# Edge layer of a four-layer graph network: GpSimd's gathers may run three groups of four columns ahead of TensorE's transposes instead of four

## The chip, the cores and the metric

The kernel runs on one core of one Trainium2 chip, in one launch. The metric is the device time of the whole program in microseconds (us). The kernel before takes 7771.75 us, the median of ten runs (7759.88 to 7787.9).

## What is computed

A graph has 12500 nodes with 32 features and 400000 edges, sorted by their target node (`dst`). Four layers run one after the other, each followed by adding its input and a layer normalisation. The change is in the third layer, which works on edges:

```python
rol, col = (edge_index[0], edge_index[1])
e_feat = jnp.concatenate([x[rol], x[col], edge_attr], axis=-1)
h = jax.nn.relu(e_feat @ W1 + b1)
v = h @ W2 + b2
x_cand = jax.ops.segment_max(v, col, num_segments=num_nodes)
return jnp.maximum(x_cand, x[:, -v.shape[-1]:])
```

So every edge needs the 32 features of its source node (random rows of a table), the 32 features of its target node (the same for a run of neighbouring edges, as they are sorted), and 32 features of its own. Then comes a small network (96 to 64 to 32), and the maximum over the edges of one target. The other three layers are sums over edges; this kernel does them as products with a dense count matrix `A`, in fp8.

## The kernel before

Edges lie as 128 partitions x 3125 columns, so that one column is 128 edges. The first 308 columns (edges of the 'heavy' targets) are treated apart, 98 blocks of them, by a generator called `heavy` (lines 1333 to 1453). The other 2817 columns are the work of `edge_layer` (line 1501 on). It takes them in three parts (`cuts`: 1984, 508 and 325 columns), each part in batches of 48 columns, each batch in **groups of four columns**. There are 705 groups; this text counts groups from 0, so group n holds the gathers number 4n+1 to 4n+4.

What a group needs, by engine and line:

- **POOL** (GpSimd) gathers the source rows, one indirect DMA for each column (`fetch`, which calls the helper at line 110): `ef<-table,ids`, 128 rows of 128 bytes. Nothing else gathers; the same engine also has to gather the results of finished parts (`ends<-scan,end_i`, 98 of them, line 110 too).
- **DVE** (VectorE) spreads the target's features over the batch with 32 scans (line 1582), and **ACT** (ScalarE) copies the edge features in (line 1578), once for each batch and one batch ahead.
- **PE** (TensorE) transposes the four columns (line 1705), DVE copies the result out of PSUM (`eT<-pT`, line 1707), PE runs the first product (lines 1736 and 1738), ACT the ReLU (line 1741), PE the second product (line 1754), ACT copies the result to `v` (line 1756).
- When a batch is through, DVE takes the running maximum with 32 scans (line 1591), and SP writes them out (`scan<-o`, 768 KB, line 1594). The next batch but one then loads `attr` (line 1562) and `begin` (line 1565), 768 KB each.

How far POOL may run ahead is set by hand. The indices of a gather are not read from `rows` directly, but from a small copy of four columns, `ids` (line 1683, on DVE). `allow` makes that copy. `AHEAD` copies are made before the loop; after that, each group's copy `eT` is followed on DVE by one further `ids` copy, that of the group `AHEAD` places later. A gather waits for its `ids`, so POOL can be at most `AHEAD` groups in front of the copy `eT`:

```python
def allow():
    if groups:
        e, k = groups.pop(0)
        ids = small.tile([P, 4], I32, name="ids", bufs=AHEAD + 2)
        nc.vector.tensor_copy(ids[:, :k], rows[:, e:e + k])
        allowed.append(ids)
...
            behind = nc.vector.tensor_copy(eT[:, :k], pT[:3 * D, :k])
            with tc.issue_after(behind.ins):
                allow()
            fill(0)
```

`fill` (called twice for each group) puts other work between: up to three steps of `heavy` for each group until its 98 blocks are done (lines 1387 to 1452; a block has its own place in every engine's queue, four groups apart), and later steps of `round_part`, that is products of the last layer with `A` (line 1320, 832 KB loads of `A` by SP). These run for nodes that the finished first or second part has already settled.

A tile framework sets the order of instructions on each engine and the semaphores. It orders by its own estimate of when things are ready; the order on an engine is then fixed, and an instruction that waits holds up all behind it on its engine.

When a part's last batch is through, `end` gathers and writes back 128 boundary rows (`fx`, `fix`), after `LEAD` further groups, and `done` gathers the `ends` and finishes nodes.

Of the kernel before, what the change touches and what calls it, by code (L numbers as in the profile page):

```python
# [119 lines left out]
def dense_path(ctx, tc, bad_i, x, src, dst, edge_attr, w1T, w1_b, w2, w2T, w2_b, aT,  # L120
# [1125 lines left out]
    with ExitStack() as st:  # L1246
# [102 lines left out]
        def heavy(hidden, outer):  # L1349
# [28 lines left out]
            for b in range(H):  # L1378
# [72 lines left out]
                for j in range(4):  # L1451
                    nc.vector.scalar_tensor_tensor(most, got[:, j, :D], lack[:, j:j + 1], most,
                                                   op0=OP.add, op1=OP.max)

        edge_layer(tc, ident, cuts, heads, edge_attr, m_W1, m_b1, m_W2, table, scan, starts_d,
                   rows_d, cont_d, psum, done, fill, lambda *a: first.append(heavy(*a)))
        while fillers:
# [43 lines left out]
def edge_layer(ctx, tc, ident, cuts, heads, edge_attr, m_W1, m_b1, m_W2, table, scan, starts_d,  # L1501
# [13 lines left out]
    C = E // P  # L1515
    HE = P * cuts[0]
    T = 48
    AHEAD = 4
    LEAD = 2 * AHEAD
    HID = m_W1.shape[1]  # L1520

    const = ctx.enter_context(tc.tile_pool(name="e_const", bufs=1))
# [79 lines left out]
    def end(s, last):  # L1602
# [30 lines left out]
        nc.scalar.copy(carry, po[:, :D])  # L1633
        yield from range(LEAD)
        fx = small.tile([P, D], F32, name="fx", bufs=1)
# [43 lines left out]
# [7 lines that stand above are left out]
    begin(lambda B, eT: hidden(nc, psum, small, mw1, mb1, B, 0, 4, eT),  # L1686
          lambda ready: outer(nc, psum, mw2, *ready))
    for _ in range(AHEAD):
        allow()
# [59 lines left out]
def outer(nc, psum, mw2, B, t, k, hT):  # L1749
    HID = P // 2  # L1750
    pv = psum.tile([P, 2, 2, D], F32, name="pv")
    if k == 4:
        for j in range(2):
            nc.tensor.matmul(pv[:, j].rearrange("p h d -> p (h d)"), hT[:, j, :], mw2,  # L1754
                             start=True, stop=True)
        nc.scalar.copy(B.v[:, t:t + 4, :].rearrange("p (h j) d -> p j h d", h=2), pv)
    else:
        for j in range(k):
            q = slice((j // 2) * HID, (j // 2 + 1) * HID)
            nc.tensor.matmul(pv[:, j % 2, j // 2, :], hT[q, j % 2, :],  # L1760
                             mw2[q, (j // 2) * D:(j // 2 + 1) * D], start=True, stop=True)
            nc.scalar.copy(B.v[:, t + j, :], pv[:, j % 2, j // 2, :])
# [660 lines left out]
```

## Time and profile before

| | |
|---|---|
| median of ten runs | 7771.75 us |
| the profiled execution | 7779.74 us |
| its span (first to last instruction) | 7777.9 us |
| edge layer: first gather of `ef` starts, last one ends | 2936.1 and 6599.4 us |
| stretch with `heavy` beside the groups | about 2936 to 4917 us |
| two stretches with products of the last layer beside the groups | within 5800 to 6280 and 6375 to 6600 us |

The profile's page gives each engine's busy time, the span in 40 slices of 194 us (a digit is the busy share in tenths; PEclk is the clock that was granted to TensorE, in tenths of full speed), and groups of instructions by line with their idle time before them and what ended it. Further views are the table by stretches of time, the list of waits, and the timeline, in which a row is: start, duration, engine, line, operation, tiles written and read, and in brackets how long the engine sat idle and what released it. For an indirect DMA, POOL's busy time is the making of its descriptors; the data lands later. 'issue' is a gap that no other engine explains.

### The profile page before, as it was taken

The numbers are of one execution on the slowest core, as the hardware profiler recorded it, in microseconds if no ns is written. First come the engines' busy times: TensorE is split into PE (matmuls) and PEld (weight loads), VectorE is DVE, ScalarE is ACT, GpSimd is POOL, SyncE is SP. The second block draws the span as 40 slices with busy tenths as digits, with TensorE's granted clock in tenths as the row PEclk, the third lists the DMA queues.
The fourth block names the chain that finished last, engine by engine and source line by source line (L and its number), as shares of the span: only waits on it lengthen the run. The fifth ranks groups of instructions, "written<-read, shape, count | busy, mean of one in ns | idle before, by whom it ended". The sixth has DMA issues, their size and how long they took to land. (4 is left out here: it accounts for less than half of the span.)

```text
span 7777.9 us, 196882 instructions
## 1 busy us (share of the span) xinstructions
PE 6710.3 (86%) x85600; PEld 5344.6 (69%) x85600; DVE 3935.2 (51%) x11040; ACT 1636.3 (21%) x3386; POOL 3514.0 (45%) x3445
## 2 busy tenths in 40 slices
PE   6788999898999997888888888678669979799998
PEld 4678999888999994555555555333335636799998
DVE  6999898795443124555555555433343343411122
ACT  1334788100000002222222222211112212100000
POOL 1003410000565527777777777777777776100000
PEclk7889999999999996767777676555569959999999
DMA  1138444889999982222222222211127726699998
GB/s 50 64 132 323 184 201 198 301 331 339 334 356 353 359 334 84 59 58 55 59 54 63 55 55 58 58 52 54 48 74 239 244 74 201 217 347 364 350 358 303
DMA packets 575180, 1447.57 MB, mean 186 GB/s; under 512 B 108408, under 2 KB 269792, under 8 KB 560864
## 3 DMA queue, kind: packets, MB, share of 16 engines
q1 hardware_dynamic: 433200, 1347.10, 47.2%
q0 software_dynamic: 110240, 66.25, 4.2%
q10 hardware_dynamic: 30864, 21.54, 0.9%
q8 instruction: 673, 11.03, 0.6%
q14 instruction: 203, 1.65, 0.1%
HBM read 1155.33 MB, written 279.27 MB: 184 GB/s over the span
## 5 line engine op out<-in xcount | busy, mean ns | idle before, releaser
L110 POOL DMA_INDIRECT ef<-table,ids x2817 | 2674.2, 949 | 884.6 <-issue 635.7
L369 PE MATMUL y<-x,a 128*128 128x96 bf16 x49980 | 2255.8, 206 | 112.9 <-issue 76.3
L369 PEld LDWEIGHTS <-a 128*128 128x128 fp8e4 x49980 | 2174.0, 98 | 142.6 <-issue 99.6
L1705 PE MATMUL pT<-ident,ef 128*96 128x128 f32 x2817 | 772.8, 357 | 571.3 <-DMA ef<-table,ids 551.6
L1705 PEld LDWEIGHTS pT<-ident,ef 128*96 128x96 f32 x2817 | 398.9, 162 | 1030.1 <-DMA ef<-table,ids 684.7
L1707 DVE COPY eT<-pT 96x512 f32<-96x512 f32 x705 | 476.1, 675 | 1065.5 <-PE pT L1705 1065.4
L983 PE MATMUL pa<-oh,ol 128*128 128x196 bf16 x4928 | 726.1, 270 | 120.3 <-DVE oh L973 77.0
L1754 PEld LDWEIGHTS pv<-mw,hT 128*128 128x128 f32 x3208 | 600.4, 261 | 266.7 <-issue 94.7
L989 ACT ACTIVATE at<-pa 128x784 uint16<-128x784 f32 x816 | 647.2, 824 | 504.9 <-PE pa L983 477.7
L277 DVE TENSOR_REDUCE v<-y 128x128 f32<-128x384 f32 (+2 forms) x152 | 83.5, 549 | 1270.5 <-PE y L271 1270.2
L1754 PE MATMUL pv<-mw,hT 128*128 128x64 f32 x3208 | 681.5, 350 | 21.0 <-ACT hT L1741 14.2
L1741 ACT ACTIVATE hT<-ph,mb 128x256 f32<-128x256 f32 x802 | 380.9, 475 | 1336.6 <-PE ph L1738 1310.0
L1019 PE MATMUL y<-x,at 128*128 128x102 bf16 x9604 | 644.8, 209 | 9.9 <-DVE x L257 5.4
L983 PEld LDWEIGHTS <-ol 128*128 128x128 bf16 x4928 | 552.5, 149 | 133.6 <-issue 78.3
L1736 PE MATMUL ph<-eT,mw 96*64 96x256 f32 x1410 | 632.7, 542 | 12.0 <-DVE eT L1707 10.6
L1738 PE MATMUL ph<-eT,mw 96*64 96x256 f32 x1408 | 632.2, 543 | 0.0
L973 DVE TENSOR_TENSOR oh<-bins_h,pl 128x1568 bf16<-128x1568 bf16 x616 | 601.1, 976 | 0.0
L1019 PEld LDWEIGHTS <-at 128*128 128x128 fp8e4 x9604 | 559.1, 98 | 23.1 <-issue 10.9
L110 POOL DMA_INDIRECT g<-code_d,ws_i x25 | 202.4, 8097 | 804.4 <-DVE ki L760 541.1
L115 POOL DMA_INDIRECT sorted_d<-hrow,pos x308 | 370.5, 1203 | 373.0 <-issue 203.6
L1320 PE MATMUL y<-a,x 128*96 128x512 fp8e4 (+1 forms) x1950 | 494.7, 390 | 1.3 <-DVE x L257 1.2
L968 DVE TENSOR_TENSOR ol<-la,lb 128x1024 bf16<-128x1024 bf16 x616 | 425.7, 693 | 72.1 <-PE pa L983 71.7
(406 smaller groups left out, 7019.2 us busy)
## 6 DMA issues: line engine op xcount, KB each, us to landing
a<-A SPq DMA_DIRECT2D x245, 3136.0 KB
A<-at SPq DMA_DIRECT2D x98, 1568.0 KB
a<-A SPq DMA_DIRECT2D x144, 832.0 KB
ef<-table,ids POOLq DMA_INDIRECT x2817
starts_d<-rows SPq DMA_DIRECT2D x44, 1024.0 KB
attr<-in_edge_attr SPq DMA_DIRECT2D x57, 768.0 KB
begin<-starts_d SPq DMA_DIRECT2D x57, 768.0 KB
scan<-o SPq DMA_DIRECT2D x57, 768.0 KB
```

The lines of the kernel that those rows point to most:

```text
L110: return nc.gpsimd.indirect_dma_start(out=o, out_offset=None, in_=tab, in_offset=IndirectOffsetOnAxis(ap=idx, axis=0))
L369: nc.tensor.matmul(y[:, q, :], block(h, q - q0), x3[:, h, :3 * F], start=(q + h == first), stop=False)
L973: nc.vector.tensor_tensor(oh, bins_h[:, None].to_broadcast([P, 4, HJ, 2]), pairs(pl[:, t, 0, half * 64 + w0:half * 64 + w0 + 8])[:, :, Non ...
L983: nc.tensor.matmul(pa[:, 2 * b + i, :HJ], ols[t][:, :, :, 4 * u + 2 * b + i].rearrange("p a b -> p (a b)"), ohs[t][:, 2 * u + b, :, i], st ...
L989: nc.scalar.activation(at[:, qd, :, off:off + 8].rearrange("p h (w j) -> p h w j", w=4), pa[:, :, :HJ].rearrange("p w (h j) -> p h w j", h ...
L1019: nc.tensor.matmul(y[0][:, q, :], at[:, q - 2 * half, h, :], x3[:, h, :3 * F0], start=(q + h == 0), stop=(c < EARLY and last and q == 2 * ...
L1320: nc.tensor.matmul(y[:3 * D, :nq * Q], x3[:, h, :3 * D], a[:, :nq, h - h0, :], start=(h == lo), stop=(h == hi - 1))
L1705: nc.tensor.transpose(pT[:3 * D, j, :], B.ef[:, t + j, :], ident)
L1707: behind = nc.vector.tensor_copy(eT[:, :k], pT[:3 * D, :k])
L1736: nc.tensor.matmul(ph[:HID, :ka], mw1, eT[:, :ka], start=True, stop=True)
L1738: nc.tensor.matmul(ph[HID:2 * HID, :k - 2], mw1, eT[:, 2:k], start=True, stop=True)
L1754: nc.tensor.matmul(pv[:, j].rearrange("p h d -> p (h d)"), hT[:, j, :], mw2, start=True, stop=True)
```

## The change

One constant goes from four to three; a second one, which was derived from it, is written out so that it stays at eight:

```diff
     T = 48
-    AHEAD = 4
-    LEAD = 2 * AHEAD
+    AHEAD = 3
+    LEAD = 8
     HID = m_W1.shape[1]
```

`AHEAD` is used in two places: the ring of `ids` buffers (`AHEAD + 2`, now five instead of six) and the number of `allow` calls before the loop (three instead of four). So the `ids` copy that follows group n's `eT` on DVE is that of group n+3 instead of n+4. No instruction is added or removed in the edge layer's arithmetic, and as many gathers are made. As the framework orders by its own estimate, the order changes with it in some places, which the built programs show: on PE 392 of 392 products of line 1447 (a late step of `heavy`) stand one to three transposes earlier than before, on POOL the `fx` gathers of the first two parts and the first eleven `ends` gathers stand four column gathers earlier, and on SP some `scan<-o` stores stand ahead of the `attr` load that they followed. On DVE the order of `eT`, `ids` and the steps of `heavy` is the same in all but a few places.

## The prediction

> **What bounds the kernel now.** I read the page's slices first, then the groups by line, then the waits of POOL, then the timeline around one batch. The page shows where the edge layer lies, and that POOL looks only three quarters busy in it:
>
> ```profile
> POOL 1003410000565527777777777777777776100000
> PEclk7889999999999996767777676555569959999999
> ```
>
> The group of the column gathers says what the other quarter is:
>
> ```profile
> L110 POOL DMA_INDIRECT ef<-table,ids x2817 | 2674.2, 949 | 884.6 <-issue 635.7
> ```
>
> A gather takes 0.949 us, and 0.314 us (884.6 / 2817) pass before each, of which most is released by nothing. That is 1.25 us for a column and 5.0 us for a group, whatever else runs: from 2936.1 to 4921.5, POOL starts 395 groups at 5.03 us each. So from 2936 to some 5960 us **POOL is the bound**, without slack: what delays a gather there delays the end. The table by stretches shows where it isn't (columns: PE, PEld, DVE, ACT, POOL busy, PEclk, DMA share, GB/s):
>
> ```profile
> 2936.00:4917.00 1981.00, 1660.87 (x8704) 1039.26 (x8705) 1072.31 (x4239) 514.10 (x1338) 1500.66 (x1577) 0.71 0.22 59
> 4917.00:5530.00 613.00, 460.86 (x1475) 227.87 (x1474) 233.46 (x932) 105.96 (x266) 463.34 (x492) 0.50 0.20 53
> 5960.00:6185.00 225.00, 225.00 (x1290) 137.88 (x1290) 84.42 (x342) 48.35 (x118) 159.70 (x170) 1.00 0.77 248
> 6480.00:6600.00 120.00, 120.00 (x713) 76.45 (x713) 40.12 (x154) 24.19 (x56) 81.11 (x86) 1.00 0.68 213
> ```
>
> In the last two rows PE is busy all the time: there PE is the bound, and POOL waits at the gate (`ids`).
>
> **The change.** It adds and removes no work. It moves one release: the `ids` that follow the copy `eT` of group n on DVE now let POOL start group n+3, not n+4. I priced it by asking of each group: when did POOL start it, and when would its `ids` have been there one place later? At the slowest place of a batch the timeline of DVE has
>
> ```profile
> 4104.36 0.68 DVE L1707 COPY eT<-pT 96x512 f32<-96x512 f32 x1
> 4105.11 0.34 DVE L1683 COPY ids<-rows 128x4 int32<-128x4 int32 x1
> 4109.72 0.69 DVE L1707 COPY eT<-pT 96x512 f32<-96x512 f32 x1 [0.87 <-PE pT L1705]
> 4110.33 0.15 DVE L1683 COPY ids<-rows 128x4 int32<-128x4 int32 x1
> ```
>
> and that of POOL
>
> ```profile
> 4103.26 0.94 POOL L110 DMA_INDIRECT ef<-table,ids  x1 [0.30 <-issue]
> ...
> 4108.26 0.94 POOL L110 DMA_INDIRECT ef<-table,ids  x1 [0.31 <-issue]
> ```
>
> Counted from the first, the `eT` copies are those of groups 229 and 230, and the gathers are the first ones of groups 232 and 233. With four ahead, the two `ids` copies release groups 233 and 234, 2.8 us early. With three ahead they are the release of 232 and 233, and come 2.2 us after POOL wanted to start (4105.45 against 4103.26; 4110.48 against 4108.26). Where POOL does wait for `ids`, it starts 0.27 us after the copy ends; so POOL loses 2.2 + 0.27 = 2.5 us here, once: the second shortfall is covered by the first.
>
> Why `eT` is late there, PE's timeline says: at the seam of two batches the 768 KB transfers `attr` and `scan<-o` start at 4086.3 and 4086.8, and the columns of group 228 land late.
>
> ```profile
> 4091.43 0.45 PE L1705 MATMUL pT<-ident,ef 128*96 128x128 f32 x1 [4.17 <-DMA ef<-table,ids]
> 4093.83 0.45 PE L1705 MATMUL pT<-ident,ef 128*96 128x128 f32 x1 [1.96 <-DMA ef<-table,ids]
> ```
>
> The last column's descriptors were done at 4087.98 and PE had it at 4093.83, 5.85 us later. PE's clock falls to 0.50 in it (from 4089 to 4110), and PE needs the next eight groups to catch up. So the shortfall comes once in a batch of 12 groups, that is 60 us.
>
> *Sum, first stretch.* Over all groups of the 33 batches beside `heavy`, start of group n against end of the `ids` copy that will be its release: in 30 batches POOL would be held, by 0.27 us more than the largest shortfall in the batch (from 0 to 2.55 us); the 30 sum to **48 us**. All of it counts only if PE, DVE and ACT are delayed with POOL; where they keep their pace, a late POOL finds the next release early. What they have in reserve is read from the time between a group's last gather and its `eT`: 1.7 to 1.8 us is the shortest in the trace (then they wait for POOL), and 13 of the 33 batches reach under 2 us, 19 under 2.7. PE waits for gathers 129 times for 260 us in this stretch, so they do follow POOL. Carrying the delay from group to group (POOL takes over the delay of its release plus the shortfall; the copies take over POOL's delay less their reserve above 1.8 us) leaves 34 us; above 2.7 us it would be 57 us; counting only the 13 batches that surely follow, 26 us. I take 41, between 34 and 48.
>
> *From 4917 to 5530* `heavy` is gone and the copies come early: the smallest reserve at three ahead is 1.56 us. Nothing. *From 5530 to 5960* 98 − 20 `ends` gathers are shared with POOL, and two groups fall short at a batch's seam, by at most 1.6 us: with the carried reserve 3 us. *5960 to 6185*: PE sets the pace, 5.2 us a group; the queue between POOL and PE gets shorter by a group (`eT` follows the last gather by 15 to 16 us there, so 10 us would be left, against 1.8 needed). Nothing inside. But when PE gets free at 6185 and POOL is the bound again, POOL is one group less far: 5.6 us, on the path. *6480 to 6600*: PE bound again to the last group; POOL's lead is worth nothing there. Nothing. After that the program is the same.
>
> *What else moves.* Five `ids` buffers instead of six: a copy waits for the gather five groups back, long done, and costs nothing. `LEAD` stays. Behind a gather that waits on POOL stand only more gathers. On DVE nothing new waits. PE's order is changed: products of line 1447 stand one or two transposes earlier. At the seam two transposes (0.32 us each) move behind them and one product of line 1736 (0.69 us) moves ahead of the last: `eT` of group 229 is between 0.6 us earlier and 0.7 later, so 33 batches make −20 to +23 us. I take nothing, as `eT` of 230, with the same shortfall, has the same order ahead of it.
>
> Sum: 41 + 3 + 5.6 = **50 us**. Against the profiled execution, 7779.74 + 50 = 7830; that execution lies 8 us above the median of the ten runs, so the time is 7771.75 + 50 = **7822 us**.
>
> **A rule that speaks against a loss.** The row is the 5.85 us above, from a column's descriptors to PE. The Trainium skill, page "DMA: Bandwidth & Descriptors", section "Anatomy of one DMA", gives a DMA from GpSimd about 2.0 us of fixed time. By that rule alone three groups in front are ample, and the sum would be nothing. The measured number decides.
>
> **Rivals.**
> 1. *No difference (within 15.5 us).* The gate binds, but not for long: PE, DVE and ACT keep their pace, so that one shortfall of some 2.8 us (2.55 + 0.27) makes room for all later ones, and with the lead lost at 6185 it is 2.8 + 5.6 = 8 us: 7780. For it: 14 batches never come under 2.7 us. Against it: PE's 260 us of waiting.
> 2. *Not slower, even faster.* The place is PE in the stretches where it is the bound and DVE's `lack` (line 1450), which waits 485 us for line 1447. If 1447, moved ahead of transposes that wait for columns, brings `eT` more than 2.5 us earlier at the seam, the gate never binds there; and POOL's waits for `ids`, 115 of 55.6 us, go down to the usual 0.30 us, which gives 21 us: 7751. It decides from 2.5 us on; I found at most 0.6.
> 3. *More.* POOL's hold makes PE idle just where it now catches up, and its clock stays at half for longer. The granted clock around here stands in stretches of 6.8, 13.7 and 20.5 us, so 3.4 us looks like its step; one more step at half in each batch costs PE 1.7 us, 33 x 1.7 = 56 us: 50 + 56 = 106, or 7878. With the upper carry (16 more) and the later `eT` (23 more) it is 7917. For it: beside `heavy` the mean clock is 0.71, so half-clock is common. Against it: the carried delays leave PE as busy per batch as before.
> 4. *The change doesn't do what it says*, as POOL never needs more than three groups: 30 batches speak against it; it would give 7772.
>
> **Chances.** A measurement of this kernel tells 0.2%, 15.5 us, from no change. Forecast (slower by 16 to 90 us) 0.70; rival 3 and what else lies beyond that 0.09; rival 1, with 4, 0.14; rival 2 0.07. So faster 0.07, same 0.14, slower 0.79. The range: its lower end is the least carry with the best order of transposes (26 − 20 = 6 us, 7777; rival 1's 7780 lies above it), its upper end rival 3 without the further terms (7878, rounded to 7880); some 0.18 is left out.
>
> **What would show it.** In the changed kernel's profile, the first stretch should be some 41 us longer (395 groups at 5.13 us instead of 5.03); POOL's waits for DVE's `ids` should grow from 115 to some 200, with waits of 1 to 2.5 us once in 60 us beside `heavy`; 4917 to 5530 should be as long as now; the tail after the last gather too. I am wrong if the waits grow but the stretch doesn't (rival 1), if `eT` at the seam comes earlier by over 1 us (rival 2), or if PE's mean clock beside `heavy` falls under 0.71 by more than 0.02 (rival 3).

## The result, and the profile after

| | before | after |
|---|---|---|
| median | 7774.28 us (30 runs) | 7833.0 us (9 runs) |
| ratio | | 1.0077, 95% interval 1.0068 to 1.0086 |
| profiled execution, span | 7777.9 us | 7829.8 us |
| edge layer: group 0 to group 395 starts | 1985.4 us | 2040.1 us |
| group 395 to 530 | 694.5 us | 694.3 us |
| copy of the last group after the first gather | 3683.7 us | 3741.8 us |

The change costs 58.7 us on the medians; a second timing of both gave 1.0071 (1.0058 to 1.0085). The two profiled executions differ by 52 us only, as the work ahead of the edge layer happened to end 9.7 us earlier in the one after (the first gather starts at 2926.4 instead of 2936.1). From the first gather on, the copy of the last group comes 58.1 us later.

The page of the kernel after, the busy slices of POOL, the clock and the group of the column gathers:

```profile
POOL 1003410000565427777777777777777776100000
PEclk7889999999999997766676677555569959999999
L110 POOL DMA_INDIRECT ef<-table,ids x2817 | 2672.5, 949 | 950.8 <-issue 667.4
```

POOL's work is the same (949 ns a gather); its idle time before gathers grew by 66 us (950.8 against 884.6). The table by stretches says where, cut at group 395 as the prediction's rows of before are, to within one group:

```profile
2926.00:4966.00 2040.00, 1724.24 (x8713) 1063.08 (x8715) 1078.82 (x4247) 513.95 (x1339) 1501.98 (x1581) 0.70 0.21 57
4966.00:5580.00 614.00, 513.74 (x1484) 240.90 (x1480) 236.47 (x939) 106.79 (x269) 464.06 (x493) 0.50 0.19 53
```

The first row holds one group more than the row 2936 to 4917 of before (1581 against 1577 instructions on POOL); counted between the same gathers, the stretch takes 55 us longer. The second is as long as before. POOL's waits in the first stretch, before and then after (columns: us in total, times, longest):

```profile
POOL ef L110 <- DVE ids L1683: 10.7, 35, 0.3
```

```profile
POOL ef L110 <- DVE ids L1683: 81.8, 100, 3.9
```

Before, an `ids` copy was never late beside `heavy` (no wait over the usual 0.3 us). After, 100 gathers wait for it, and 71 us more in all. Most of the 100 are waits of the usual 0.3 us that some other row had before. Read gather by gather, 32 waits exceed 0.45 us, and what they have above the usual 0.3 us sums to 56.6 us, about what the stretch grew by. They lie in 19 of the 33 batches, nearly all at the first gather of a batch's fifth or sixth group; the other 14 batches lose nothing.

The seam shown in the prediction looks like this afterwards. POOL, then DVE:

```profile
4118.90 0.94 POOL L110 DMA_INDIRECT ef<-table,ids  x1 [0.31 <-issue]
4122.69 0.94 POOL L110 DMA_INDIRECT ef<-table,ids  x1 [2.84 <-DVE ids L1683]
...
4127.90 0.94 POOL L110 DMA_INDIRECT ef<-table,ids  x1 [0.52 <-DVE ids L1683]
```

```profile
4112.37 0.15 DVE L1683 COPY ids<-rows 128x4 int32<-128x4 int32 x1
4121.50 0.69 DVE L1707 COPY eT<-pT 96x512 f32<-96x512 f32 x1 [1.37 <-PE pT L1705]
4122.26 0.15 DVE L1683 COPY ids<-rows 128x4 int32<-128x4 int32 x1
4126.87 0.69 DVE L1707 COPY eT<-pT 96x512 f32<-96x512 f32 x1 [0.86 <-PE pT L1705]
4127.48 0.15 DVE L1683 COPY ids<-rows 128x4 int32<-128x4 int32 x1
```

The gather at 4122.69 is the first of group 232, the one that the prediction named. It waits 2.84 us, of which 0.3 are usual: 2.5 us are lost. The next group, at 4127.90, loses 0.2 more. The copies are late because columns are, as before; PE's timeline at the seam (group 228):

```profile
4109.93 0.45 PE L1705 MATMUL pT<-ident,ef 128*96 128x128 f32 x1 [4.63 <-DMA ef<-table,ids]
```

Which batches are held goes with how late columns are: the last column of the batch's first group reaches PE 5.3 us after its descriptors were done in the 19 (3.0 to 6.1), and 1.9 us in the others (1.3 to 4.0; batch 0 left out, means and extremes).

One thing is different at the seam: the order on PE. The end of group 229's four transposes, before and then after:

```profile
4101.31 1.75 PE L1447 MATMUL z<-ends,last 128*128 128x33 f32 x8
4102.88 1.04 PE L1393 MATMUL y<-one,key 128*128 128x128 bf16 x8
4103.72 0.42 PE L1705 MATMUL pT<-ident,ef 128*96 128x128 f32 x1
```

```profile
4119.40 0.63 PE L1705 MATMUL pT<-ident,ef 128*96 128x128 f32 x2
4119.96 1.12 PE L1736 MATMUL ph<-eT,mw 96*64 96x256 f32 x2
4121.01 0.45 PE L1705 MATMUL pT<-ident,ef 128*96 128x128 f32 x1
```

A product of line 1736 (two records, 1.12 us at half clock) now stands ahead of the group's last transpose. From the last transpose of group 228 to that of group 229 PE takes 11.1 us, where it took 9.9 before (4109.93 to 4121.01; 4093.83 to 4103.72). It is 11.1 us in each of the 19 held batches, and was 9.9 us in each of the 16 batches of before whose last column took over 4 us.

### The profile page after: what moved, and what is told of

The parts are those of the page before. It is cut to its first block, busy times and chain, and to the rows that moved or that the text cites. A ratio compares the mean times of both kernels' runs of the same rounds, so it can differ in the third digit from the quotient of the medians.

```text
span 7829.8 us, 196864 instructions
## 1 busy us (share of the span) xinstructions
PE 6817.8 (87%) x85600; PEld 5372.1 (69%) x85600; DVE 3940.5 (50%) x11040; ACT 1635.8 (21%) x3386; POOL 3510.7 (45%) x3445
## 5 line engine op out<-in xcount | busy, mean ns | idle before, releaser
L110 POOL DMA_INDIRECT ef<-table,ids x2817 | 2672.5, 949 | 950.8 <-issue 667.4
L1705 PE MATMUL pT<-ident,ef 128*96 128x128 f32 x2817 | 803.4, 361 | 521.3 <-DMA ef<-table,ids 517.7
L1754 PEld LDWEIGHTS pv<-mw,hT 128*128 128x128 f32 x3208 | 619.4, 267 | 289.3 <-issue 102.9
L1754 PE MATMUL pv<-mw,hT 128*128 128x64 f32 x3208 | 716.2, 359 | 29.9 <-ACT hT L1741 24.0
L1736 PE MATMUL ph<-eT,mw 96*64 96x256 f32 x1410 | 641.3, 549 | 9.8 <-DVE eT L1707 8.9
L1738 PE MATMUL ph<-eT,mw 96*64 96x256 f32 x1408 | 642.0, 550 | 0.0
```

The source lines that it names most:

```text
L110: return nc.gpsimd.indirect_dma_start(out=o, out_offset=None, in_=tab, in_offset=IndirectOffsetOnAxis(ap=idx, axis=0))
L1705: nc.tensor.transpose(pT[:3 * D, j, :], B.ef[:, t + j, :], ident)
L1736: nc.tensor.matmul(ph[:HID, :ka], mw1, eT[:, :ka], start=True, stop=True)
L1738: nc.tensor.matmul(ph[HID:2 * HID, :k - 2], mw1, eT[:, 2:k], start=True, stop=True)
```

## The experiments

The **theory** is that of the prediction: three groups in front are too few at the seams of the batches beside `heavy`, because 1.5 MB of transfers there make columns land late and PE then works at half clock, and too few by a group at the end of the first stretch where PE is the bound. The **rivals** are that the changed order of instructions costs the time; that the seam's own work, and not the transfers, makes the copies late; and that a longer lead always helps, or a shorter one always costs. The first four kernels, and the last four, ran on chips where the kernel before takes 7773 and 7777 us. The four between ran on a chip where it takes 9067 us.

**Two groups.** Edit: `AHEAD = 2`, `LEAD = 8`.

> AHEAD = 2, LEAD stays 8. Theory (late release at the seams): the shortfalls of the kernel before, read with two groups of lead, are up to 11.5 us where three groups gave up to 2.55 beside heavy, and even the median group is short. Carried from group to group as in the prediction, with a reserve counted above 1.8 us or above 2.7 us, the end is 259 to 328 us later than with four; so 8030 to 8105 us, with most of it (213 to 268 us) before the group 395. Rival (the changed order of instructions costs the time, and the release itself little): no rule says that the order gets steadily worse, so about what three ahead cost, 7800 to 7870 us.

Measured: 8050.12 us, ratio 1.0355 (1.0336 to 1.0374), 277 us more. Up to group 395 the stretch is 210 us longer, at the last copy 266 us. The end is where the carried shortfalls put it (259 to 328, near the lower end), the stretch 3 us short of its range (213 to 268). A cost that steps from 0 to 59 to 277 us, as the shortfalls read from the trace of the kernel before say, speaks for the release. It doesn't exclude the order by itself, as the order moves too: the products of line 1447 stand five to seven transposes earlier here than before.

**Three and a half groups.** The `ids` of a group are copied in two halves, each with its own place in the queue of releases (against the kernel after; the main lines):

```diff
-    AHEAD = 3
+    AHEAD = 7
...
-            e, k = groups.pop(0)
-            ids = small.tile([P, 4], I32, name="ids", bufs=AHEAD + 2)
-            nc.vector.tensor_copy(ids[:, :k], rows[:, e:e + k])
+            e, k, o = groups.pop(0)
+            if o == 0:
+                held[:] = [small.tile([P, 4], I32, name="ids", bufs=6)]
+            ids = held[0][:, o:o + k]
+            nc.vector.tensor_copy(ids, rows[:, e:e + k])
...
-                allow()
+                for j in range(0, k, 2):
+                    allow()
```

> The release goes by half groups of two columns, seven halves ahead, so POOL may be three and a half groups in front. Theory (late release): half a group is 2.5 us of POOL's time, and the largest shortfall at three groups was 2.55 us, so beside heavy almost every shortfall is gone: the stretch up to group 395 takes within 8 us of what it took with four ahead, and at the end of the stretch where PE is the bound half of 5 us is lost: 7774 to 7786 us. Rival (the order): the order lies between those of three and four groups, and the time with it, about 7795 to 7815 us.

Measured: 7784.73 us, 1.0014 (1.0004 to 1.0023), 12 us more; up to group 395, 9.9 us more. The time is in the theory's range and the stretch 2 us over it. Half a group, 2.5 us of POOL's time, brings back 47 of 59 us. The rival's 7795 is excluded by the interval (its upper end is 7791). But the rival's condition didn't come about: the order at the seam is that of four groups here (776 of the 784 records of line 1447 stand where they stood before). So this run took away late release and changed order together, and can't tell one from the other.

**No loads of `attr`, with three groups and with four.** The features of the first batch's edges are used for all batches, so both leave out 56 of 57 loads:

```diff
-            self.at = work.tile([P, T, D], F32, name="attr", bufs=1)
-            nc.sync.dma_start(self.at.rearrange("p t d -> p (t d)")[:, :n * D],
-                              of_stage(edge_attr, s)[:, cols])
+            self.at = attr0
```

> AHEAD = 3, and the edges' own features are loaded once for the first batch and used for all batches, so 56 of the 57 loads of 768 KB are left out (the computation of the other batches uses the wrong features). Theory (the transfers at the seam make the columns land late, and only there is the release late): half of the burst of 1.5 MB is gone, some 3.5 us of it at 214 GB/s, more than any shortfall, so beside heavy at most a fifth of the 55 us remains: 7774 to 7795 us. Rival (the seam's own work on PE, DVE and ACT, or the order, makes the copies late): as with the loads, 7820 to 7840 us.

> The control of the run with three ahead and without the loads of the edges' own features: AHEAD = 4, the same loads left out. Both theories: POOL is the bound beside heavy already, and one DMA load less changes nothing for it, so 7760 to 7778 us, and the stretch up to group 395 as long as before (1985 us) within 5 us.

Measured: with three groups 7783.21 us, 1.0018 (1.0009 to 1.0027); with four 7771.67 us, 0.9997 (0.9987 to 1.0007). Both lie in the theory's ranges. With three, the stretch up to group 395 is 2.3 us longer than before instead of 55, with four 4.2 us, so that beside `heavy` three groups now cost nothing against four. POOL's waits in that stretch, of the kernel with three:

```profile
POOL ef L110 <- DVE ids L1683: 22.7, 59, 1.5
```

59 waits of mostly the usual 0.3 us. The last column of a batch's first group reaches PE 2.1 us after its descriptors (mean over the batches; 3.9 in the kernel after), and the copies of the second group follow their last gather by 7.8 us, where it was 10.2 before and 9.7 after. So it is the transfers at the seam that three groups can't ride out. And the order of three groups by itself, which this kernel keeps (line 1447 as in the kernel after), costs no more than these 2 us when little is late.

The two kernels still differ by 11.5 us, all of it after group 395: against the kernel before, the one with three loses 3.4 us there up to the last copy, the one with four gains 9.5. No run says why the latter gains.

The clock is told by the same stretch of the two kernels, three and then four:

```profile
2929.00:4917.00 1988.00, 1743.59 (x8715) 1078.66 (x8715) 1080.68 (x4249) 511.56 (x1338) 1501.38 (x1581) 0.69 0.17 45
```

```profile
2918.00:4908.00 1990.00, 1757.89 (x8715) 1094.07 (x8715) 1078.28 (x4250) 512.58 (x1338) 1508.33 (x1581) 0.68 0.17 45
```

It is lower than before (0.71) and after (0.70), and yet next to nothing is lost. So a low mean clock alone doesn't make POOL wait.

**Three groups only after `heavy`.** Four are allowed up to group 399, then one release is skipped:

```diff
+            shown.append(t)
             behind = nc.vector.tensor_copy(eT[:, :k], pT[:3 * D, :k])
             with tc.issue_after(behind.ins):
-                allow()
+                if not 400 <= len(shown) < 401:
+                    allow()
```

> Four groups ahead up to group 399, three from there on. On a chip where the kernel before takes about 7770 us: up to group 395 as before within 3 us, and 5 to 9 us lost after it, 7776 to 7786 us. Rival (the loss is spread over the whole edge layer, or lies in the order after heavy): 7795 us or more. On a chip where it takes about 9070 us: no difference, as in the earlier run there (0.9993).

Measured: 7779.45 us, 1.0003 (0.9994 to 1.0012). Up to group 395 0.7 us more; the last copy 5.9 us later. Of this, 4.7 us come between groups 631 and 650, where PE stops being the bound: about the 5.6 us of the prediction, in one profile; the medians (2.5 us, interval −5 to +9) can't tell it from nothing. The rival is out: almost all of the loss lies beside `heavy`.

**The changed kernel once more.**

> The changed kernel once more, beside the kernel before on the same chip. On a chip where the kernel before takes about 7770 us: 1.0077 as before, within 0.002. On a chip where it takes about 9070 us, the theory expects next to nothing, 0.998 to 1.004: there POOL is held at the gate with four, five and seven groups alike, as something behind PE sets the pace, and a shorter queue starves nobody so long as the copies follow the last gather by 15 us and more. Rival (three ahead costs a fixed 60 us wherever it runs): 1.0065.

Measured: 7835.08 us, 1.0071 (1.0058 to 1.0085). Up to group 395 2041.2 us, 55.8 more than before; last copy 59.8 us later. So the profile of the kernel after was no accident.

**Seven groups.** The `ids` lie in one ring tile (against the kernel after):

```diff
-    AHEAD = 3
+    AHEAD = 7
...
+    ring = const.tile([P, 12, 4], I32, name="ring")
...
-            ids = small.tile([P, 4], I32, name="ids", bufs=AHEAD + 2)
+            ids = ring[:, allowed_n[0] % 12]
+            allowed_n[0] += 1
```

> AHEAD = 7, the ids in one ring tile of twelve groups, LEAD 8. On a chip where the kernel before takes about 7770 us: POOL's waits at the gate in the first stretch with PE as the bound are 12 us above the usual gaps, and at most these are won: 7758 to 7773 us; if a longer queue costs something elsewhere, 7780 to 7800 us. On a chip where it takes about 9070 us: 1.002, as in the earlier run there.

Measured: 7757.73 us, 0.9976 (0.9965 to 0.9987): 19 us faster than with four, and faster than both kernels. Up to group 395 3.1 us less, as expected about nothing; at the last copy 16.9 us less. The time is just under the range. Where it comes from, the table shows by the stretch from group 590 to 631, before and with seven:

```profile
5966.00:6184.00 218.00, 218.00 (x1253) 133.92 (x1251) 82.05 (x334) 47.47 (x116) 154.65 (x164) 1.00 0.77 247
```

```profile
5962.00:6167.00 205.00, 205.00 (x1177) 125.71 (x1176) 75.46 (x300) 45.02 (x109) 154.82 (x165) 1.00 0.77 247
```

POOL gets through the same 164 gathers in 205 us, not 218, while PE is as busy: it no longer waits at the gate for PE. When PE is free again, POOL is 13 us further.

**A busy seam.** To see the clock's part, PE gets something to do while columns are late:

```diff
             for j in range(k):
+                for _ in range(10 if t == 0 and j else 0):
+                    nc.tensor.matmul(pT[3 * D:, j, :], ident[:, :D], ident, start=True, stop=True)
                 nc.tensor.transpose(pT[:3 * D, j, :], B.ef[:, t + j, :], ident)
```

> AHEAD = 3; in front of the last three transposes of each batch's first group PE does ten small products each (128 x 32 by 128 x 128, float32) into unused rows of the same PSUM tile; the result is not touched. On a chip where the kernel before takes about 7770 us: if the half clock after the seam is what keeps the copies late, the granted clock beside heavy rises above 0.75, the copies of the second and third group of a batch come 2 us earlier or more, and the time falls to 7780 to 7810 us; if the late landing alone sets them, the copies come as late or later by the 3 us of added work, 7825 to 7900 us. On a chip where it takes about 9070 us: some 4% slower, as in the earlier run there, and no answer.

Measured: 7846.82 us, 1.009 (1.0072 to 1.0109). The time lies in the range of the second answer, 7825 to 7900; the signs inside the stretch are those of the first. The two stretches say how that goes together:

```profile
2930.00:4927.00 1997.00, 1827.72 (x10697) 1184.82 (x10697) 1095.42 (x4253) 511.66 (x1340) 1500.84 (x1582) 0.79 0.22 58
5992.00:6265.00 273.00, 273.00 (x1639) 174.91 (x1638) 87.47 (x348) 51.92 (x128) 173.59 (x185) 1.00 0.70 221
```

Beside `heavy` the clock is 0.79 (0.70 in the kernel after), the copies of a batch's second and third group follow their last gather by 7.8 and 7.0 us (means; 9.7 and 10.0 after), and the stretch takes 1996 us: 44 of the 55 us are back, with more work. That fits the half clock. But where PE is the bound, the added products cost time: against the kernel before, 67 us more at the last copy than at group 395, which I had left out of the expected time. And the order moved here too: the framework put steps of `heavy` in front of the last columns' transposes, so that from the last transpose of a batch's first group to that of its second PE takes 3.7 us here, 11.1 at the held seams after. That work was done while the columns were late. How the 44 us divide between clock and order, this run can't tell.

**Five, seven, three after `heavy`, and the busy seam, on the chip with 9067 us.**

> AHEAD = 5 with six ids buffers, LEAD 8. Theory (late release): beside heavy POOL is not held with four groups and can't gain there; at the end of the first stretch where PE is the bound POOL is one group further, so up to 5 us less at the end: 7764 to 7774 us, the stretch up to group 395 as before within 5 us. Rival (more lead is always better, or the order costs): a change of the stretch beside heavy by 10 us or more, either way.

> AHEAD = 7, the ids in one ring tile of twelve groups, LEAD 8. Theory: POOL's waits at the gate in the first stretch with PE as the bound are 12 us above the usual gaps in the kernel before; at most these are won: 7760 to 7773 us. If a longer queue in front of PE costs something (gathers of the part's ends that stand behind more column gathers on POOL, say), it is slower than with four: 7780 to 7800 us.

> Four groups ahead up to group 399, three from there on (one ids copy is skipped). Theory: up to group 395 as before within 3 us; after it only the 5 us at the end of the first stretch with PE as the bound, and some 3 us at the seams around the ends gathers: 7776 to 7786 us. Rival (the loss is spread over the whole edge layer, or lies in the order after heavy): 7795 us or more.

> AHEAD = 3; in front of the last three transposes of each batch's first group PE does ten small products each (128 x 32 by 128 x 128, float32) into unused rows of the same PSUM tile, so that it has something to do while columns are late; the result is not touched. If the half clock after the seam is what keeps the copies late, the granted clock beside heavy rises above 0.75, the copies of the second and third group of a batch come 2 us earlier or more, and the time falls to 7780 to 7810 us. If the late landing alone sets them, the copies come as late or later by the 3 us of added work: 7825 to 7900 us.

Measured there: 1.0011 (0.9997 to 1.0025), 1.0023 (1.0008 to 1.0039), 0.9993 (0.9978 to 1.0008) and 1.0378 (1.0341 to 1.0414). The expected times don't apply, as they start from 7774. The page of the kernel with five groups:

```profile
L110 POOL DMA_INDIRECT ef<-table,ids x2817 | 2667.3, 947 | 1865.1 <-DVE ids L1683 880.4
```

On this chip POOL isn't the bound: it is held at the gate with five groups, with seven (copies 40 us behind the gathers) and with four (21 us; the kernel with three only after `heavy`, up to there) alike. PE, DVE and ACT set the pace, at 6.6 us a group, and a lead is worth nothing. Five groups were not run on a chip with 7770 us.

## Why the prediction was right

It forecast slower, 7822 us (7777 to 7880); 7833.0 was measured. The sign, the place and what POOL waits for hold. The size is 9 us short on the medians (50 forecast, 58.7 measured), and that it came so near is in part luck, as the terms show.

- *POOL is the bound beside `heavy`, and a late release there is lost.* Right: the stretch grew by 55 us, the next one by none, and POOL's long waits at the gate sum to about that (56.6 us).
- *The release of group 232 comes 2.2 us late, 2.5 us are lost, the second shortfall is covered.* Right at that very seam (2.5 us, and 0.2 at the next group). That the number agrees is some luck: PE's order alone makes that copy 1.2 us later than in the trace of the kernel before (next but one point).
- *Sum of the first stretch: 41 us.* The mis-sized term: 54.6 and 55.8 us in two profiles. The prediction had 30 batches held, by 1.6 us each on the mean (48 / 30) and 2.8 at most, and then took off what PE, DVE and ACT have in reserve. In the profile 19 batches are held, by 3.0 us each on the mean, and 14 not at all; in the second profile 17, by 3.3 us. Fewer and longer holds gave nearly the same sum. Nor does the carry of 57 stand for a bound: it is more than the 48 in which all shortfalls count, because above 2.7 us as a reserve it lets a copy be later than POOL is. Worked again without that, it is 44.
- *PE's order, put at nothing.* This is the step that failed. It read the moved product of line 1736 as 0.69 us; its two records take 1.12 us, and at every held seam PE needs 1.2 us longer from the last transpose of a batch's first group to that of the second (11.1 us; 9.9 at the late seams of before). As an estimate, 19 times 1.2 us make some 23 of the 56.6 us. At the other seams, where the second group's columns are the late ones, the copy of the second group comes earlier instead: it follows its last gather by 7.0 us on the mean, while before it was 8.1 us at the least from batch 2 on. That fits an order in which the steps of `heavy` run ahead of the late columns, as *rival 2* had it. No run has three groups with the order of four, so how the 55 us divide between the order and the lead itself stays open; with few late columns the two together cost 2.3 us (the run without loads).
- *4917 to 5530: nothing.* Right (694.3 and 694.5 us from group 395 to 530).
- *5530 to 5960: 3 us; then 5.6 us where PE is freed.* POOL lost 3.8 us in the first, but the copies didn't follow (they were 2 us nearer). At the end of PE's stretch they came 5.1 us later, and 4.7 us in the kernel with three groups after `heavy` only. From group 395 to the last copy the loss is 3.5 us (4.0 in the second profile, 5.3 in that kernel) instead of 8.6, and the last stretch gives next to nothing, as said.
- *PE's clock.* That the half clock after the seam makes the copies late was an argument from one row. The busy seam fits it, but its order moved too; and without the loads the mean clock was lower still, with next to nothing lost. The clock's share isn't shown.
- *Rival 1* fails by the stretch, *rival 2* as a whole by the interval, *rival 4* by the 32 long waits. *Rival 3*'s sign was a clock lower by over 0.02 beside `heavy`; it fell from 0.71 to 0.70.
- *The signs.* The waits for `ids` grew from 115 to 187 over the whole layer (some 200 expected), and 5.16 us a group (2040.1 / 395) stand against 5.13. The 2.0 us of the Trainium skill's page "DMA: Bandwidth & Descriptors", section "Anatomy of one DMA", by which nothing would have been lost, are near what a column needs away from the late seams (1.9 us on the mean from descriptors to PE in the batches that weren't held) and far under what it needs at them (5.3 us).

## What to carry to other kernels

A queue that runs ahead of the bound engine is sized by the worst place, not by the mean: here three groups covered the median release by 3.6 us, and missed the seam by some 3 us in 19 of 33 batches. It can be priced without running it: for each release, compare the time when the engine started with the time when the release one place later came, and add up what is short, by period. If the change also moves the order on another engine, price that by whole products (all their records, at the clock of that place): the term put at nothing here was 1.2 us at each late seam. A longer lead pays where the bound changes engines: the lead gathered while another engine is the bound is kept.

## What the runs showed of the hardware that was not expected

- Beside two 768 KB transfers at a seam, a column of 16 KB was with PE 5.85 us after its descriptors were done; in batches that weren't held it took 1.9 us on the mean. Without one of the two transfers the mean over the batches was 2.1 us instead of 3.9.
- PE's clock stays at 0.50 for some 20 us (4089 to 4110) after waits of 4.17 and 1.96 us at such a seam. Giving PE 30 small products there raised the mean from 0.70 to 0.79. What that is worth isn't shown: the kernels without the loads had 0.69 and 0.68 and lost only 2.3 and 4.2 us beside `heavy`.
- One chip ran the kernel before in 9067 us, 17% over the others. With five groups there, group 0 to 395 took 2628 us instead of 1985 (2617 with four), and the work after the last copy 1158 us as elsewhere (1158 us before). A gather lasts as long (947 ns); what grew are waits that the trace puts to no instruction ('remote'), 2421 us in all on ACT and DVE in this profile and none in that of the kernel before, such as

```profile
DVE lack L1450 <- remote: 343.7, 33, 12.6
```

  (us in total, times, longest). What makes them wasn't found.
